# A two-layer kernel with routed experts: a later place for the third sequence's shared experts, and a group-wise scatter of layer 1's rows

## The chip, the core and the metric

The kernel runs on one core of one Trainium2 chip. The metric is the device time of one execution in microseconds (us). The engines that matter here are the TensorE (PE in the profile; PEld is its loading of weights), the VectorE (DVE), the ScalarE (ACT), the GpSimd (POOL) and the SyncE (SP), which only starts transfers. Each engine executes its own instructions in order, and waits for others by semaphores. [...]

## The reference

Four sequences of 1024 tokens of 256 numbers pass through two layers. In each, a mixer gives s and a feed-forward part gives g, both from the same normalized input, and x becomes x + s * silu(g):

```python
x = L0_attn_x
xn = _layernorm(x)
s = _L0_attn_ref(xn, ...)          # minGRU, a scan over the tokens
g = _silu(_L0_ffn_ref(xn, ...))    # 16 experts of 128 hidden, 4 of them per token
x = x + s * g
xn = _layernorm(x)
s = _L1_attn_ref(xn, ...)          # attention on cos(theta) * cos(xn)
g = _silu(_L1_ffn_ref(xn, ...))    # shared experts + 16 experts of 64 hidden, 4 per token
x = x + s * g
```

The two parts of layer 1 that the change touches are, with x standing for the normalized input:

```python
# attention of one sequence
proj = cos(theta) * cos(x)
out  = softmax(proj @ proj.T / sqrt(16)) @ proj @ W_c.T + b_c
# feed-forward of one sequence
shared = (silu(x @ shared_gate_w.T) * (x @ shared_up_w.T)) @ shared_down_w.T   # 512 hidden
routed = sum over the 4 chosen experts e of  w_e * (silu(x @ gate_e) * (x @ up_e)) @ down_e
g      = silu(shared + routed)
```

Attention and the shared experts of a sequence need nothing of the routed experts; the three meet in the last line of the layer only.

## The kernel before

**Tiles.** Rows are taken 128 at a time, one token to a partition. A sequence has 8 such tiles and is worked on in two halves of four tiles. All matrix products are in float32.

**Routed experts of layer 1.** The sequences form two groups, (0, 1) and (2, 3). For a group, `route1` (L895) normalizes the rows, writes them to `normed` in DRAM, computes the router's products and picks the four experts of each token. `places1` (L920) then gives each of its (token, expert) pairs a slot, so that the slots of one expert lie together. `dispatch1` (L923 to L945) reads the normalized rows back, half a sequence at a time (`t_half`, L938), adds the pairs' numbers (L939, L940), and scatters the rows into the slots in DRAM with `scattered` (L569 to L579): 16 indirect DMAs for each half sequence, all started by POOL (L574), 64 for a group. Loads run two halves ahead of the scatters (AHEAD = 2), and `t_half` takes one of the 8 buffers of a pool (tag "x", XB = 8) that serve the rows gathered in layer 0, the values of the attention and the results of the experts as well. `weights1` (L947) turns the weights of a group's pairs into weights by slot on DVE (L447, L454, L455).

`experts1` (L1166) goes through the slots of both groups, 20 quads of four tiles for each. `experts` (L588) loads a quad with ACT's queue (L613), transposes it (`turn`, L622, L626), multiplies with an expert's weights (`hidden`, L634), transposes (`turn_hidden`, L651) and multiplies again (`down`, L659). `store` scatters the results with indirect DMAs of POOL (L1192).

**Attention, shared experts, gating.** `prep1` (L954 to L1003) computes the cosines and the products of the values (L993, copied to `val` by ACT at L1000). `attend` (L1005 to L1108) is the attention of one sequence: scores (L1046), exponentials (L1058, L1062), products with the values (L1078); the last blocks are copied by DVE and ACT (L1103, L1105). `share` (L1114 to L1164) does the shared experts of one sequence: the two products with the 512 hidden (L1125), the sigmoid part on ACT (L460), two products on DVE (L461, L1135), the product back (L1141), then ACT's copy (L1161) and write to `shared` in DRAM (L1162). `gated1` (L1208 to L1261) waits for a group's results, loads `shared`, `attended` and the four results of each token, adds them up (L1231) and finishes the layer (L1246 to L1249).

**Order.** The order is written out at build time. `run(steps, us, beside)` emits one main stage step by step and moves a modelled clock on by `us` for each step; after each step it lets the side stages in `beside` emit those steps that are due by that clock. A side stage (`Beside`) is a generator that yields how long it wants to pause. So the modelled clock decides where side work stands among the main work on each engine; at run time the engines follow their orders and semaphores alone. `pool_free` is the modelled time at which POOL will have started all its indirect DMAs, at 1.27 us each (INDIRECT). `together` and `until` move the clock on without main work; `behind` puts what is emitted inside it behind all that has been emitted so far on each engine.

Layer 0's experts are the first main stage that matters here, with four side stages: `clearing` (zeros into the slots), `combined` (the last scan, and layer 0's gathers and gating, `combine0`, with the gathers at L716 and the gating at L782, L789 and L791), `routing` and `preparing`. `routing` holds, one after the other, the routes and places of group 0, those of group 1, and both dispatches. Then follow attention and shared experts of the sequences 0, 1 and 2, then all routed experts of layer 1, then the shared experts and the attention of sequence 3:

```python
others = [clearing, combined, routing, weighing]
for b in range(3):
    preparing = Beside(prep1(b + 1, "gu")) if b < 2 else Beside(())
    run(attend(b), ATTEND, [*others, preparing])
    run(share(b), SHARE, [*others, preparing])
    together(preparing)
```

Of the kernel before, what the change touches and what calls it, by code (L numbers as in the profile page):

```python
# [26 lines left out]
GROUPS = ((0, 1), (2, 3))  # L27
# [26 lines left out]
PAIR, ATTEND, SHARE, ROUTED = 0.81, 1.4, 2.6, 0.64  # L54
# [8 lines left out]
def two_layer_kernel(  # L63
# [33 lines left out]
    def halves(dram, b):  # L97
        return dram[b].rearrange("(c p) d -> p c d", p=P)
# [380 lines left out]
    G1 = len(GROUPS)  # L479
# [80 lines left out]
    def spent(us):  # L560

        clock[0] += us
# [282 lines left out]
    @contextmanager  # L845
    def behind():

        with ExitStack() as stack:
            engines = mybir.EngineType
            for engine in (engines.PE, engines.DVE, engines.Activation, engines.SP, engines.Pool):  # L850
                stack.enter_context(tc.issue_after(latest(engine)))
            yield
# [21 lines left out]
    def run(steps, us, beside=(), until=None):  # L874


        for i, _ in enumerate(steps, 1):
            clock[0] += us
            for other in beside:
                with behind():  # L880
                    other.advance(clock[0])
            if i == until:
                break
# [37 lines left out]
        placed1.append((yield from places(em1[:, tiles_of(h), :], G1 + h, WE1, "tp")))  # L921

    def dispatch1(h):  # L923
        while not clearing.done:
            yield PIECE
        row, top, _ = placed1[h]
        pieces = [(b, q) for b in GROUPS[h] for q in range(NQ)]
        n = NS * TOPK
        views = dram_disjoint_views(rows_in[G1 + h], len(pieces) * n)

        tokens = {}
        for i in range(-AHEAD, len(pieces)):
            if i + AHEAD < len(pieces):
                j = i + AHEAD
                tokens[j] = t = xpool.tile([P, NS, D + INFO], F32, tag="x", name="t_half", bufs=XB)
                ts = slice(j * NS, (j + 1) * NS)
                b, q = pieces[j]
                nc.gpsimd.dma_start(out=t[:, :, 0:D], in_=halves(normed, b)[:, q * NS : (q + 1) * NS, :])  # L938
                nc.gpsimd.tensor_copy(t[:, :, D : D + TOPK], top[:, ts, 0:TOPK])  # L939
                nc.gpsimd.tensor_copy(t[:, :, D + TOPK], result0[:, ts])  # L940
            if i >= 0:
                scattered(views[i * n : (i + 1) * n], tokens.pop(i), row, i * NS)
                while clock[0] < pool_free[0] - n * INDIRECT:
                    yield PIECE
        dispatched.add(h)  # L945
# [8 lines left out]
    def prep1(b, tag):  # L954

        if b < 2:
            while b not in turned:
                yield PIECE
            xnT = turned[b]
        else:  # L960
            while b not in routed_done:
                yield PIECE
            xnT = transposed_tile()
            nc.sync.dma_start(out=xnT.rearrange("p k s -> p (k s)"), in_=normedT[b])
            there = clock[0] + LANDING
            while clock[0] < there:
                yield PIECE
        if b == 1:

            projT = [work.tile([P, QUAD, D + INFO], F32, tag="q", name="projT", bufs=QB) for _ in range(KC)]  # L970
            projT = [t.rearrange("p i d -> p (i d)")[:, 0:S] for t in projT]
        else:
            projT = work.tile([P, KC, S], F32, tag="big_a", name="projT", bufs=1)
            projT = [projT[:, kc, :] for kc in range(KC)]
        for kc in range(KC):
            for cols in (slice(0, TB), slice(TB, S)):
                k = work.tile([P, TB], F32, tag="t", name="k", bufs=1)
                for _ in cos_reduced(projT[kc][:, cols], xnT[:, kc, cols], k, TWO_PI_NORMED):
                    pass
                yield 2 * PIECE  # L980
        for kc in range(KC):
            nc.scalar.activation(projT[kc], projT[kc], AF.Sin, bias=half_pi, scale=-1.0)
        yield PIECE
        for kc in range(KC):
            nc.vector.tensor_scalar(projT[kc], projT[kc], cth[:, kc : kc + 1], None, ALU.mult)
        yield 3 * SETTLED

        val = [xpool.tile([P, NS, D + INFO], F32, tag="x", name="val", bufs=XB)[:, :, 0:D] for _ in range(NQ)]
        for c in range(0, NT, 2):
            ps = bank(tag, 2)  # L990
            for i in range(2):
                for kc in range(KC):
                    nc.tensor.matmul(  # L993
                        ps[:, i * D : (i + 1) * D],
                        lhsT=projT[kc][:, (c + i) * P : (c + i + 1) * P],
                        rhs=wc_sb[:, kc, :],
                        start=(kc == 0),
                        stop=(kc == KC - 1),
                    )
            nc.scalar.copy(val[c // NS][:, c % NS : c % NS + 2, :], ps.rearrange("p (c d) -> p c d", d=D))  # L1000
            spent(1.7)
            yield PIECE
        ready[b] = xnT, projT, val  # L1003
# [162 lines left out]
    def experts1():  # L1166

        views = [dram_disjoint_views(r, n) for r, n in zip(results, NSLOT[G1:])]

        def target(q, xs):  # L1170

            info = xs[:, :, D:]
            own = slot_no[:, q * QUAD : (q + 1) * QUAD]
            nc.vector.scalar_tensor_tensor(
                info[:, :, 0:TOPK],
                info[:, :, 0:TOPK],
                -MARK,
                own.unsqueeze(2).to_broadcast([P, QUAD, TOPK]),
                ALU.add,
                ALU.is_gt,  # L1180
            )
            to_row = small.tile([P, QUAD, 1], F32, tag="to_row", name="to_row", bufs=1)
            nc.vector.tensor_reduce(to_row, info, AX.X, ALU.add)

            dest = small.tile([P, QUAD], I32, tag="dest", name="dest", bufs=6)
            nc.vector.scalar_tensor_tensor(dest, own, float(B * S * TOPK), to_row[:, :, 0], ALU.add, ALU.min)  # L1186
            return dest

        def store(g, q, o, dest):
            indirect(QUAD)  # L1190
            for i in range(QUAD):
                nc.gpsimd.indirect_dma_start(  # L1192
                    out=views[g - G1][QUAD * q + i],
                    out_offset=bass.IndirectOffsetOnAxis(ap=dest[:, i : i + 1], axis=0),
                    in_=o[:, i, :],
                    in_offset=None,
                )

        def begin(g):
            until(lambda: g - G1 in dispatched, routing, weighing)  # L1200

        def end(g):
            stored1[g - G1] = max(clock[0], pool_free[0]) + LANDING

        of_tiles = [of_tile for _, _, of_tile in placed1]
        return experts(range(G1, 2 * G1), of_tiles, we1_sb, WE1, P // 2, store, target, begin, end)

    def gated1(b):  # L1208
# [104 lines left out]
    def then(*steps):  # L1313
        for g in steps:
            yield from g

    def until(ready, *beside):

        while not ready():
            clock[0] += PIECE  # L1320
            for other in beside:
                with behind():
                    other.advance(clock[0])

    ready, turned, placed1, weights, dispatched, stored1 = {}, {}, [], [], set(), {}
    clearing = Beside(clears(10))
    combined = Beside(then(gru(xnTs[3], 3, ("side", "side"), True), *(combine0(g) for g in range(len(HALVES)))))
    routing = Beside(
        then(
            *(step for h, bs in enumerate(GROUPS) for step in (routes1(bs, "side"), places1(h))),  # L1330
            *(dispatch1(h) for h in range(len(GROUPS))),
        )
    )
    preparing = Beside(prep1(0, "side"))
    with behind():
        run(experts0(), PAIR, [clearing, combined, routing, preparing])
# [9 lines left out]
    nc.sync.dma_start(out=we1_sb, in_=w1)  # L1346
    combined.pace = routing.pace = 0.7
    weighing = Beside(weights1())
    others = [clearing, combined, routing, weighing]
    for b in range(3):  # L1350
        preparing = Beside(prep1(b + 1, "gu")) if b < 2 else Beside(())
        run(attend(b), ATTEND, [*others, preparing])
        run(share(b), SHARE, [*others, preparing])
        together(preparing)
    until(lambda: len(placed1) == len(GROUPS), *others)
    preparing = Beside(prep1(3, "gu"))

    gating = Beside(then(*(gated1(b) for b in range(B))), 1.7)
    with behind():
        run(experts1(), ROUTED, [routing, weighing, preparing, gating])  # L1360
    together(preparing, weighing)
    gating.pace = 1.0
    run(share(3), SHARE, [gating])
    run(attend(3), ATTEND, [gating])
    together(gating)

# [64 lines left out]
```

## Time and profile before

| what | time |
| --- | --- |
| median of five runs | 1479.96 us |
| lowest and highest of the five | 1464.4 and 1483.38 us |
| the profiled execution | 1485.71 us |
| its span on the core | 1483.7 us |

| engine | busy us | share of the span | instructions |
| --- | --- | --- | --- |
| PE | 1095.3 | 74% | 4928 |
| DVE | 648.9 | 44% | 1963 |
| POOL | 552.5 | 37% | 588 |
| ACT | 464.0 | 31% | 1030 |

In the profiled execution layer 0's gathers end at 776 us. Group 0 of layer 1 is scattered from 803 to 888 us, group 1 from 909 to 991 us. attend(2) starts at 1003 us and share(2) at 1051 us; the routed experts of layer 1 start at 1098 us. share(3) follows them from 1384 us on and attend(3) from 1427.5 us on. The last matmul ends at 1475.3 us.

The profile comes from one execution. It gives, for each engine, busy time and the groups of instructions that make it up; for each stretch of time, busy time, granted clock and DMA traffic; and, for every instruction, when it ran, how long its engine was idle before it, and what ended that idle time. The chain of waits follows the work that ended last back from the last instruction, at each step to what released it. "remote", in the chain "another core or an unknown queue", stands for an idle time whose end the profile can't put down to an instruction.

### The profile page before, as it was taken

How to read it: one execution, taken by the hardware profiler on the slowest of the kernel's cores; microseconds unless marked ns; L12 is line 12 of the kernel's file. 1: busy time of each engine (PE TensorE's matmuls, PEld its weight loads, DVE VectorE, ACT ScalarE, POOL GpSimd, SP SyncE). 2: the span in 40 equal slices, each digit the busy share in tenths (PEclk: the TensorE clock that was granted, in tenths of full speed). 3: DMA queues.
4: the chain of work that ended last, by engine and by line, in shares of the span. 5: the costliest groups of instructions: out<-in, count | busy, mean ns of one | idle time of the engine just before them, and what ended most of it. 6: DMA issues, size and time to landing. Idle time of an engine off the chain costs nothing.

```text
span 1483.7 us, 16138 instructions
## 1 busy us (share of the span) xinstructions
PE 1095.3 (74%) x4928; PEld 809.5 (55%) x4928; DVE 648.9 (44%) x1963; ACT 464.0 (31%) x1030; POOL 552.5 (37%) x588
## 2 busy tenths in 40 slices
PE   6537751399928999939688718319989898879997
PEld 4215321288827878626366504207667676667566
DVE  5813910233317853137958314111244333546585
ACT  3404420244414554302333301002225444434222
POOL 0570277300264000266243774750005555546300
PEclk9756775599959999968799759759999989879999
DMA  9982334288948959838254433320224456887681
GB/s 337 401 328 91 102 116 146 93 219 226 268 136 243 282 165 242 281 104 198 73 199 157 158 106 116 117 79 15 85 78 147 158 163 195 274 274 235 211 269 54
DMA packets 154290, 264.81 MB, mean 178 GB/s; under 512 B 14176, under 2 KB 118752, under 8 KB 152928
## 3 DMA queue, kind: packets, MB, share of 16 engines
q1 hardware_dynamic: 106976, 137.18, 30.8%
q0 software_dynamic: 27264, 75.86, 15.0%
q10 hardware_dynamic: 19968, 50.75, 10.2%
q8 instruction: 43, 0.70, 0.2%
q14 instruction: 39, 0.32, 0.1%
HBM read 119.34 MB, written 144.39 MB: 178 GB/s over the span
## 4 chain that ended last, share of the span: by engine, by line
PE 39%; another core or an unknown queue 18%; DVE 15%; issue 11%; POOL 9%; DMA 4%; ACT 2%; ACTq 0%; POOLq 0%; DVEq 0%; SPq 0%
PE gu L634 9%; POOL results L1192 6%; PE acc L659 5%; PE acc L1078 4%; PE tp L622 3%; POOL r L716 3%; PE gu L1125 2%; PE acc L1141 2%; PE mm L1046 2%; PE mm L1125 2%; DMA xs<-rows_in 2%; PE tp L651 1%; PE acc L288 1%; DVE stats L191 1%
## 5 line engine op out<-in xcount | busy, mean ns | idle before, releaser
L716 POOL DMA_INDIRECT r<-rows_out,row x128 | 127.6, 997 | 371.8 <-DMA g_half<-in_x_dram 146.9
L634 PE MATMUL gu<-w_sb,xT 128*128 x1280 | 255.7, 346 | 3.2 <-issue 3.1
L1192 POOL DMA_INDIRECT results<-o,dest x160 | 159.0, 994 | 243.2 <-DVE dest L1186 171.3
L634 PEld LDWEIGHTS gu<-w_sb,xT 128*128 128x128 f32 x1280 | 208.9, 206 | 19.8 <-issue 4.4
L461 DVE SCALAR_TENSOR_TENSOR h<-sg,gu 128x256 f32<-128x256 f32 (+1 forms) x160 | 56.3, 352 | 359.8 <-ACT sg L460 311.9
L659 PE MATMUL acc<-w_sb,hT 128*128 (+1 forms) x640 | 182.4, 408 | 2.2 <-ACT hT L653 1.3
L574 POOL DMA_INDIRECT rows_in<-x_half,row x128 | 128.3, 1002 | 144.9 <-issue 95.2
L622 PE MATMUL tp<-ident,xs 128*128 128x128 f32 x640 | 108.8, 296 | 75.2 <-ACT xT L626 41.0
L1078 PE MATMUL acc<-val,es 128*128 128x256 f32 x512 | 132.9, 406 | 33.0 <-ACT es L1058 22.2
L626 ACT COPY xT<-tp 128x512 f32<-128x512 f32 x160 | 94.0, 587 | 166.6 <-PE tp L622 60.1
L622 PEld LDWEIGHTS tp<-ident,xs 128*128 128x128 f32 x640 | 79.1, 150 | 114.8 <-issue 51.6
L574 POOL DMA_INDIRECT rows_in<-t_half,row x128 | 125.8, 983 | 39.3 <-issue 36.7
L1078 PEld LDWEIGHTS acc<-val,es 128*128 128x128 f32 x512 | 100.8, 204 | 59.9 <-ACT es L1058 24.4
L659 PEld LDWEIGHTS acc<-w_sb,hT 128*128 128x128 f32 (+1 forms) x640 | 114.1, 198 | 31.6 <-issue 19.8
L1141 PE MATMUL acc<-w_sb,act 128*128 128x256 f32 x256 | 64.9, 403 | 57.0 <-DVE act L1135 37.8
L651 PE MATMUL tp<-ident,h 128*128 128x128 f32 (+1 forms) x320 | 65.9, 290 | 52.7 <-issue 40.0
L460 ACT ACTIVATE sg<-gu 128x256 f32<-128x256 f32 (+1 forms) x160 | 53.1, 332 | 161.0 <-PE gu L634 95.7
L1141 PEld LDWEIGHTS acc<-w_sb,act 128*128 128x128 f32 x256 | 51.0, 202 | 77.2 <-DVE act L1135 36.5
L651 PEld LDWEIGHTS tp<-ident,h 128*128 128x128 f32 (+1 forms) x320 | 40.2, 133 | 68.2 <-issue 48.6
L1046 PE MATMUL mm<-projT 128*128 128x512 f32 (+3 forms) x192 | 72.9, 504 | 0.0
L1125 PE MATMUL mm<-xnT,w_sb 128*128 128x512 f32 x128 | 63.0, 616 | 9.3 <-DVE act L461 9.3
L653 ACT COPY hT<-tp 128x256 f32<-128x256 f32 (+1 forms) x160 | 58.4, 365 | 27.2 <-remote 8.4
(224 smaller groups left out, 1503.0 us busy)
## 6 DMA issues: line engine op xcount, KB each, us to landing
rows_in<-zeros SPq DMA_DIRECT2D x20, 1044.0 KB
xs<-rows_in ACTq DMA_DIRECT2D x40, 522.0 KB
xs<-rows_in SPq DMA_DIRECT2D x40, 512.0 KB
rows_out<-o ACTq DMA_DIRECT2D x40, 512.0 KB
r<-results SPq DMA_DIRECT2D x32, 512.0 KB
rows_in<-zeros SPq DMA_DIRECT2D x1, 12288.0 KB
rows_in<-zeros SPq DMA_DIRECT2D x1, 8192.0 KB
w_sb<-in_w_dram SPq DMA_DIRECT2D x4, 1536.0 KB
```

What stands on the lines that cost most here:

```text
L574: nc.gpsimd.indirect_dma_start(out=view, out_offset=bass.IndirectOffsetOnAxis(ap=row[:, c0 + s, k : k + 1], axis=0), in_=tokens[:, s, :], ...
L622: nc.tensor.transpose(tp[:, at : at + P], xs[:, j % per * 2 + i, kc * P : (kc + 1) * P], ident)
L626: nc.scalar.copy(xT.rearrange("p i k t -> p (i k t)"), tp)
L634: nc.tensor.matmul(ps[:, i * 2 * hid : (i + 1) * 2 * hid], lhsT=xT[:, i, kc, :], rhs=w_sb[:, bass.ds(off + kc * 2 * hid, 2 * hid)], start= ...
L651: nc.tensor.transpose(tp[0:hid, i * P : (i + 1) * P], h[:, i, :], ident)
L659: nc.tensor.matmul(ps[:, i * D : (i + 1) * D], lhsT=hT[0:hid, i * P : (i + 1) * P], rhs=w_sb[0:hid, bass.ds(expert(2 * j + i) + 4 * hid, D ...
L716: nc.gpsimd.indirect_dma_start(out=r[:, k, :], out_offset=None, in_=rows_out[g], in_offset=bass.IndirectOffsetOnAxis(ap=row[:, c, k : k + ...
L1046: nc.tensor.matmul(ps[:, at:TB], lhsT=projT[kc][:, t * P : (t + 1) * P], rhs=projT[kc][:, q * TB + at : (q + 1) * TB], start=(kc == 0), st ...
L1078: nc.tensor.matmul(av[s // 2][:, (s % 2) * D : (s % 2 + 1) * D], lhsT=es[:, s * P : (s + 1) * P], rhs=val[t // NS][:, t % NS, :], start=(t ...
L1125: nc.tensor.matmul(ps, lhsT=w[:, kc, j * P : (j + 1) * P], rhs=xr[:, kc, :], start=(kc == 0), stop=(kc == KC - 1),)
L1141: nc.tensor.matmul(ys[s // 2][:, (s % 2) * D : (s % 2 + 1) * D], lhsT=h[:, s * P : (s + 1) * P], rhs=ds1_sb[:, j, :], start=(j == 0 and s ...
L1192: nc.gpsimd.indirect_dma_start(out=views[g - G1][QUAD * q + i], out_offset=bass.IndirectOffsetOnAxis(ap=dest[:, i : i + 1], axis=0), in_=o ...
```

## The change

Three things are changed. First, `dispatch1` is taken out of `routing` and becomes a side stage of its own, `dispatching`. Group h is dispatched as soon as the slots are cleared, layer 0's side work (`combined`, the last gathers in it) has been emitted and the places of group h have been emitted; before, both dispatches came behind the routes and places of both groups. Second, share(2) is left out of the loop over the first three sequences. Third, it is emitted behind the routed experts of layer 1, ahead of share(3). The number of instructions stays the same.

```diff
     def dispatch1(h):
-        while not clearing.done:
+
+        while not (clearing.done and combined.done and len(placed1) > h):
             yield PIECE
...
         def begin(g):
-            until(lambda: g - G1 in dispatched, routing, weighing)
+            until(lambda: g - G1 in dispatched, dispatching, weighing)
...
             *(step for h, bs in enumerate(GROUPS) for step in (routes1(bs, "side"), places1(h))),
-            *(dispatch1(h) for h in range(len(GROUPS))),
         )
     )
+    dispatching = Beside(then(*(dispatch1(h) for h in range(len(GROUPS)))))
...
-    others = [clearing, combined, routing, weighing]
+    others = [clearing, combined, routing, dispatching, weighing]
     for b in range(3):
         preparing = Beside(prep1(b + 1, "gu")) if b < 2 else Beside(())
         run(attend(b), ATTEND, [*others, preparing])
-        run(share(b), SHARE, [*others, preparing])
+        if b < 2:
+            run(share(b), SHARE, [*others, preparing])
         together(preparing)
...
     with behind():
-        run(experts1(), ROUTED, [routing, weighing, preparing, gating])
+        run(experts1(), ROUTED, [dispatching, weighing, preparing, gating])
     together(preparing, weighing)
     gating.pace = 1.0
-    run(share(3), SHARE, [gating])
+    for b in (2, 3):
+        run(share(b), SHARE, [gating])
     run(attend(3), ATTEND, [gating])
     together(gating)
```

## The prediction

> **What bounds the kernel now.** I read the busy table of the page, then the busy time by stretches of time, then the chain of waits and the timelines of ACT, PE and POOL between 735 and 1110 us, where the moved work lies. Two stages matter: POOL's issue of layer 1's row scatters, and what follows the routed experts.
>
> Busy time by stretches (columns: stretch, its length, busy us and instruction count of PE, PEld, DVE, ACT, POOL, then granted clock, DMA share, GB/s):
>
> ```profile
> 803.00:888.00 85.00, 41.01 (x166) 31.44 (x163) 32.32 (x108) 17.93 (x37) 65.78 (x70) 0.70 0.41 143
> 909.00:991.00 82.00, 35.24 (x102) 20.95 (x100) 10.96 (x22) 2.99 (x5) 62.81 (x67) 0.75 0.35 124
> 1050.00:1092.00 42.00, 41.44 (x131) 24.50 (x129) 17.93 (x33) 7.68 (x13) 0.00 (x0) 1.00 0.19 63
> 1387.00:1422.00 35.00, 35.00 (x108) 20.22 (x108) 19.18 (x34) 6.73 (x12) 4.81 (x5) 1.00 0.81 262
> 1422.00:1475.00 53.00, 52.31 (x226) 39.04 (x224) 34.21 (x70) 17.43 (x54) 0.00 (x0) 1.00 0.46 151
> ```
>
> In the first two, group 0 and group 1 are scattered, and PE works less than half the time though it has share(1), the projection of values and the end of attend(1) to do. In the third, share(2) now runs, and PE is full. In the last two, share(3) and attend(3) run after the experts, and PE is full too.
>
> The chain of waits (start, us, what) says what holds PE in the first two:
>
> ```profile
> 844.36 4.99 PE gu L993 x16
> 849.64 34.04 another core or an unknown queue
> 884.29 9.91 another core or an unknown queue
> ...
> 926.00 7.67 another core or an unknown queue
> 933.72 18.89 another core or an unknown queue
> 952.66 43.35 another core or an unknown queue
> ...
> 999.60 3.78 PE acc L1141 x8
> 1003.38 3.58 PE mm L1046 x8
> ```
>
> The ACT timeline names the waiting instructions (start, duration, last bracket: idle time before, releaser):
>
> ```profile
> 883.70 0.59 ACT L1000 COPY val<-gu 128x512 f32<-128x512 f32 x1 [33.74 <-remote]
> ...
> 933.69 0.60 ACT L460 ACTIVATE sg<-mm 128x512 f32<-128x512 f32 x1 [7.12 <-remote]
> 952.63 0.60 ACT L460 ACTIVATE sg<-mm 128x512 f32<-128x512 f32 x1 [18.34 <-remote]
> 996.03 0.60 ACT L460 ACTIVATE sg<-mm 128x512 f32<-128x512 f32 x1 [42.80 <-remote]
> ```
>
> Each of these reads a PSUM tile that PE had filled long before; with one core there is no other core to wait for. What arrives late is PE's completion signal, and it does so while POOL issues indirect DMAs without a pause: group 0's 64 at one per 1.27 us from 803.29 to 887.6, group 1's 64 from 909.0 to 990.9. The wait grows with the time since the run of scatters began: 7 us at 25 us into it, 18 at 44, 43 at 87. In group 0's run the last handoff that passes is at about 40 us, and the next release comes at 883.70, 80 us in. When POOL stops, PE is full again (47.00 of 47 us from 1003).
>
> **Moving share(2).** Before it stands between attend(2), whose last matmul ends at 1050.85, and the first transpose of the experts at 1097.61: 46.76 us. The PE timeline shows the end of it:
>
> ```profile
> 1087.82 3.62 PE L1141 MATMUL acc<-w_sb,act 128*128 128x256 f32 x16
> 1097.61 1.97 PE L622 MATMUL tp<-ident,xs 128*128 128x128 f32 x8 [6.17 <-DMA xs<-rows_in]
> ```
>
> So PE works on share(2) for 40.6 us (1050.85 to 1091.44), then waits 6.17 us for the experts' first rows. That wait does not go with share(2): the experts' rows are loaded from ACT's queue (L613), behind ACT's last copy. After the change that is attend(2)'s L1105 (0.59 us), and the load takes the 4.77 us that the chain shows: a new gap of 5.7 us, between 0 (the load gets ahead of the copy) and 6.2. Gain: 46.76 - 5.7 = 41.0 us. The experts cannot be held by their data when they start 41 us sooner: the scatter of group 1 ends at 990.9, 60 us before 1050.85, and POOL does nothing from then to 1111.35. The weights of group 1 (DVE, 12 instructions of 0.42 us, 5.0 us) then lie beside attend(2), where DVE is busy 3.14 of 47 us.
>
> Afterwards the same 64 products of L1125 and 64 of L1141 run behind the experts. The price is that of share(3): its second half runs from 1406.86 to 1427.50, 20.64 us with no idle time, so 41.3 us for two halves. Nothing covers it: PE is busy 35.00 of 35 us there, and attend(3) follows at full PE. The 41.3 us are paid in full; the lower bound is share(2)'s present 40.6, the upper some 3 us more if its DVE work (16 instructions of 0.69 us, 11 us) lies badly with gated1's (in that stretch DVE is busy 19.18 of 35). Its 8 + 4 ACT instructions (0.60 us each, 7 us) have room. gated1(2) must now wait until share(2)'s two writes have landed (SP's loads of shared for it, and gated1(3)'s loads queued behind them, wait too); but DVE has 125 us of PE time in the tail for work that now fits in 84, so the end stays attend(3)'s last matmul plus the 8.4 us of finishing (1475.3 to 1483.7). Sum of this part: -41.0 + 41.3 = +0.3, between -6 and +4.
>
> **Group 0's scatter.** Before, group 0 is dispatched after both groups' routing, and three loads of rows (L938) stand on POOL ahead of the first scatter. POOL's timeline:
>
> ```profile
> 786.56 0.81 POOL L938 DMA_DIRECT2D t_half<-normed  x1 [10.54 <-DVE pen L327]
> ...
> 792.45 0.80 POOL L938 DMA_DIRECT2D t_half<-normed  x1 [4.74 <-DVE cden L347]
> ...
> 801.80 0.75 POOL L938 DMA_DIRECT2D t_half<-normed  x1 [8.23 <-DVE y L782]
> ...
> 803.29 1.05 POOL L574 DMA_INDIRECT rows_in<-t_half,row  x1 [0.16 <-POOL t_half L940]
> ```
>
> The three loads take buffers that the last three pieces gathered in layer 0 give back (L782, ends near 786.3, 792.2 and 801.5). In the new order one load takes an earlier piece's buffer, the second the one free at 786.3, and scatters stand between the second and the third. So the first scatter comes at about 788.5, 13 to 15 us sooner, and the last near 874 instead of 887.6. The instructions on POOL are the same in number. places1(1) (first matmul L362 at 896.73) stands on PE behind the value projection, so what counts is when L362 runs; group 1's scatter follows it by 12 us (909.0), and share(1)'s remainder and attend(2) follow that.
>
> How much of the 13 us comes through? The releases should keep their distance from the start of the run of scatters. The last handoff passes at 40 to 44 us, now about 831, and the next at 80 us, now about 869. At 831 PE stands 18 us of work before the 849.6 where it stopped in the profile (attend(1) ended at 844.15 and L993 at 849.4). It does that after 869, to 887, then the remaining value products (3.78 and 2.08 us): L362 near 893, 4 us earlier. If instead nothing more is caught than before, it is 13 us earlier; if attend(1) is caught 30 us in (where the second run already shows waits of 7 to 18 us), 27 us and more of work is left at 874 and L362 comes at up to 910, 13 us late. I take -4, with both ends for the range. The 12 weight instructions of group 0 (5.0 us), now ahead of share(1)'s second half on DVE, fall into waits of 18 to 43 us and cost 0; without that cover 5.
>
> One rule speaks against any effect here. The Trainium skill, "SBUF — State Buffer", section "Who interferes with whom", says that PE and ACT never wait on anyone for SBUF, only GpSimd and DVE share a port pair. If that were all, POOL's scatters would not hold PE's handoffs, their shift would be worth 0, and the whole would be +0.3. The 42.80 us row above does not look like that; no other row here separates a memory port from a late signal.
>
> **Sum.** +0.3 - 4 = -3.7 us on the profiled execution of 1485.71 us (span 1483.7), 1482.0. That execution is 5.75 us above the median of 1479.96, so the median becomes 1476. The five times before lie between 1464.4 and 1483.38, so 1% (15 us) is about what can be told from no change.
>
> **Rivals.** A, faster: the end of the scatter alone sets L362, so the whole 13 us come through, and the experts' first load is hidden too: -13 to -18, 1462 to 1467. For it: 883.70 and 996.03 both lie at the end of a run. Against it: attend(1) is not done when the signals begin to stay out. B, slower: the last 25 us of attend(1) and the route of sequence 3, many short PE-ACT-DVE handoffs, fall 15 us deeper into the run. It decides if attend(1) has not ended by 880 us; L362 then comes 13 us late or more, group 1's run and its 80 us with it, and with share(1)'s first half (918 before) caught as well up to 25 us: 1493 to 1505. For it: waits of 7 us appear 25 us into a run. Against: attend(1) ran 817 to 842, 14 to 39 us into its run, with one stall of 4.46 us. C, the new conditions do not act: the gathers and L782 set the first scatter as before (three loads waited for them), leaving only +0.3: 1480.
>
> **Chances.** Forecast 0.46 (own range 1466 to 1489), A 0.22, B 0.24, C 0.08. Faster by over 1% (under 1465): most of A and an edge of the forecast, 0.23; slower (over 1495): most of B and an edge, 0.25; else 0.52. For 8 in 10 the range takes A to 1455 (A's end less half of the spread of the times) and B to 1503.
>
> **What would show it.** Right: experts' first transpose 5 to 7 us after attend(2)'s last matmul; share(2) and share(3) as some 81 us of full PE after the experts; first scatter near 788; L362 near 893; attend(2) starting near 999. A would show L362 near 884, B one after 905 and attend(1) ending after 870. The forecast is wrong if the scatter costs PE nothing once it is moved, or if PE idles in the tail because gated1 holds buffers that share(2) needs.

## The result and the profile after

| | before | after |
| --- | --- | --- |
| median of all executions | 1483.6 us (79 runs) | 1478.24 us (42 runs) |
| lowest and highest | 1460.22 and 1504.78 | 1463.77 and 1493.83 |
| profiled execution | 1485.71 us, span 1483.7 | 1473.43 us, span 1471.7 |

The ratio of after to before is 1.0003, with a 95% interval of 0.9981 to 1.0025: no change that can be told. This ratio leaves out executions more than 1.5% above the fastest of their kernel (48 of 79 before, 9 of 42 after), which here cuts into an ordinary spread with a standard deviation of some 9 us; the medians of all executions stand at 0.9964. The forecast of -3.7 us (0.9975) lies between the two and just outside the interval. Its two terms were both wrong in size, in opposite directions, as the profile after shows.

Busy time by stretches, after (columns as before: stretch, length, busy us and count of PE, PEld, DVE, ACT, POOL, granted clock, DMA share, GB/s): the scatter of group 0, that of group 1, then share(2) and share(3) behind the experts.

```profile
785.00:873.00 88.00, 52.14 (x220) 39.31 (x218) 42.84 (x151) 23.26 (x50) 68.92 (x74) 0.81 0.47 163
895.00:978.00 83.00, 37.38 (x110) 21.91 (x108) 16.21 (x33) 5.38 (x9) 63.15 (x67) 0.74 0.33 114
1328.00:1372.00 44.00, 41.86 (x131) 24.46 (x130) 21.24 (x36) 8.72 (x15) 5.17 (x6) 1.00 0.36 118
1372.00:1416.00 44.00, 41.84 (x123) 23.74 (x123) 28.71 (x54) 8.46 (x15) 0.00 (x0) 0.96 0.64 203
```

PE still works only half of the time beside the scatters. The tail is not quite full: PE misses 2 us in each of the last two stretches, where before it was busy 35.00 of 35.

The chain of waits, after (start, us, what):

```profile
852.61 25.68 another core or an unknown queue
878.31 0.60 ACT val L1001
...
878.96 5.40 PE gu L994 x12
884.35 0.43 PE tp L362 x2
...
911.08 8.66 another core or an unknown queue
919.79 14.06 another core or an unknown queue
933.89 42.66 another core or an unknown queue
976.57 0.60 ACT ysh L1162
```

The same unexplained waits stand at the same kind of place as before, the two ahead of L362 having become one of 25.68 us instead of 34.04 and 9.91. ACT's timeline names them:

```profile
878.31 1.07 ACT L1001 COPY val<-gu 128x512 f32<-128x512 f32 x2 [25.39 <-remote]
...
933.87 0.60 ACT L460 ACTIVATE sg<-mm 128x512 f32<-128x512 f32 x1 [13.51 <-remote]
976.57 0.60 ACT L1162 ACTIVATE ysh<-acc 128x512 f32<-128x512 f32 x1 [42.10 <-remote]
```

POOL's last scatter of group 0 ends at 872.8, that of group 1 at 977.8; both long waits end near the end of a run of scatters, not at a fixed time from its start (878.31 is 92.8 us behind the first scatter of its group, 976.57 is 81.0).

Marks of the two timelines, in us (the first column is the end of layer 0's gathers on POOL):

| | gathers end | first scatter | L362 | attend(2) ends | experts start | last L659 ends | last matmul ends |
| --- | --- | --- | --- | --- | --- | --- | --- |
| before | 776.0 | 803.3 | 896.7 | 1051.0 | 1097.6 | 1387.9 | 1475.3 |
| after | 773.7 | 785.5 | 884.2 | 1032.2 | 1036.0 | 1328.5 | 1463.2 |

From these differences: -2.3 us up to the gathers, which the change doesn't touch; -10.2 from the gathers to L362 and -6.3 from there to the end of attend(2), together -16.5 for the dispatch; -42.8 from attend(2) to the experts, +2.2 in the experts and +47.3 behind them, together +6.7 for the move of share(2). The sum is -12.1, in two single executions of kernels that scatter by some 9 us each: the one of before took 2.1 us more than the median of its kernel, the one of after 4.8 us less.

### The profile page after: what moved, and what is told of

It is laid out like the page before. It is cut to its first block, busy times and chain, and to the rows that moved or that the text cites. A ratio compares the mean times of both kernels' runs of the same rounds, so it can differ in the third digit from the quotient of the medians.

```text
span 1471.7 us, 16132 instructions
## 1 busy us (share of the span) xinstructions
PE 1084.6 (74%) x4928; PEld 804.9 (55%) x4928; DVE 649.3 (44%) x1963; ACT 463.2 (31%) x1030; POOL 558.8 (38%) x588
## 3 DMA queue, kind: packets, MB, share of 16 engines
q10 hardware_dynamic: 19968, 50.75, 10.2%
## 5 line engine op out<-in xcount | busy, mean ns | idle before, releaser
L634 PE MATMUL gu<-w_sb,xT 128*128 x1280 | 252.7, 343 | 0.8 <-issue 0.8
L659 PE MATMUL acc<-w_sb,hT 128*128 (+1 forms) x640 | 183.6, 410 | 0.7 <-ACT hT L653 0.7
L659 PEld LDWEIGHTS acc<-w_sb,hT 128*128 128x128 f32 (+1 forms) x640 | 114.9, 200 | 30.2 <-issue 17.7
```

What stands on the lines that cost most here:

```text
L634: nc.tensor.matmul(ps[:, i * 2 * hid : (i + 1) * 2 * hid], lhsT=xT[:, i, kc, :], rhs=w_sb[:, bass.ds(off + kc * 2 * hid, 2 * hid)], start= ...
L659: nc.tensor.matmul(ps[:, i * D : (i + 1) * D], lhsT=hT[0:hid, i * P : (i + 1) * P], rhs=w_sb[0:hid, bass.ds(expert(2 * j + i) + 4 * hid, D ...
```

## Experiments

Times on different chips were of two kinds: the kernel before took some 1170 us on four chips and 1480 to 1500 us on three, the latter like the recorded comparison. So each comparison below is with runs of before on the same chip, and each says which kind of chip it was: with PE's signals late (as in the profiles shown so far), or not. A signal is the semaphore update by which an engine tells a waiting one that its work is done.

**The two halves of the change alone.** Only share(2) moved (shown against the changed kernel; the lists of side stages have `routing` again in place of `dispatching`):

```diff
 def dispatch1(h):
-    while not (clearing.done and combined.done and len(placed1) > h):
+    while not clearing.done:
...
+            *(dispatch1(h) for h in range(len(GROUPS))),
-    dispatching = Beside(then(*(dispatch1(h) for h in range(len(GROUPS)))))
```

> Only share(2) is moved; the dispatch stays as before. Theory (the move is a wash: some 41 us less ahead of the experts, 41 us plus a loss to gated1's DVE work more behind them): the median stays within 5 us of the kernel before; the experts' first transpose comes 41 to 47 us sooner than before; share(2) and share(3) take 82 us if nothing is in their way, 87 us if gated1's DVE bursts cost what they cost in the changed kernel (87.7 us there, against two times 20.64 x 2 = 82.6). Rival (the move itself gains, the dispatch nothing): 8 to 12 us under before, as in the changed kernel's profile.

Only the dispatch changed (against the changed kernel):

```diff
-        if b < 2:
-            run(share(b), SHARE, [*others, preparing])
+        run(share(b), SHARE, [*others, preparing])
...
-    for b in (2, 3):
-        run(share(b), SHARE, [gating])
+    run(share(3), SHARE, [gating])
```

> Only the dispatch is changed; share(2) stays in the loop. Theory (what moves the time is the earlier scatter): L362 comes near 884 us instead of 897, attend(2) starts 10 to 20 us sooner, and the median is 5 to 12 us under before. Rival (the starved stretch takes it back, the shift is run-to-run scatter): within 4 us of before, with attend(2) ending at its old place.

Both fell on a chip without late signals: before 1171.21 us, the move alone 1188.04 us (ratio 1.014, interval 1.0103 to 1.0178), the dispatch alone 1167.63 us (0.9969, 0.9943 to 0.9995). The move was expected to be a wash and lost 17 us; the dispatch gained 3.6 us, less than its theory and within what its rival allowed. L362 stood at 669.4 and 667.8 there; the numbers expected for it belonged to the other kind of chip.

**The kernel before and the changed kernel on such chips.**

> The kernel before, unchanged, for its profile on the chip of the first experiments. The executions there were 300 us shorter than those of the first profile, with a granted clock of 0.94 instead of 0.85. Theory: PE's completion signals are not late on this chip; the scatters of group 0 and group 1 then end near 800 us with PE busy over 80% beside them, and no wait of ACT for a remote releaser over 5 us. Rival: another part of the kernel is faster there, and the waits of 18 to 43 us under the scatters are still in it.

> The changed kernel, unchanged. Theory (share(2) in the loop hid the end of group 1's scatter, which holds the results' scatters on POOL when the experts start 40 us sooner): on the chip of the first experiments 0.5 to 1.2% over before, with the experts stopped for 15 to 30 us some 36 us after their start, and share(2) + share(3) taking 84 to 88 us. On a chip with late signals: within 1% of before. Rival (only gated1's DVE bursts cost): 0.3 to 0.5% over before, no stop in the experts.

The kernel before took 1172.34 us in its profiled execution, and the changed kernel 1180.78 us against 1169.95 us (ratio 1.0084, 1.0051 to 1.0117). Busy time beside the whole run of scatters (632.9 to 806.8 us), kernel before on a chip without late signals:

```profile
632.90:806.80 173.90, 164.38 (x644) 112.66 (x642) 78.55 (x228) 46.73 (x111) 133.44 (x143) 0.99 0.49 166
```

POOL issues the same 128 scatters at the same 1.27 us each, and PE is busy 95% of the time instead of some 45%; no wait in this profile is put down to a remote releaser. So the scatters as such, with their bytes and their place, do not hold PE.

With late signals, the waits are not the dispatch's alone. In the trace of before 25 waits of 3 us or more are put down to a remote releaser, 349 us in all (some beside each other), and each begins in a run of at least 12 of POOL's indirect DMAs with less than 1 us between one and the next. Layer 0's scatters and gathers are among these runs; ACT's timeline:

```profile
286.20 0.59 ACT L626 COPY xT<-tp 128x512 f32<-128x512 f32 x1 [26.93 <-remote]
...
664.90 0.60 ACT L1058 ACTIVATE es<-mm 128x512 f32<-128x512 f32 x1 [21.37 <-remote]
```

The first wait began in a run of 80 scatters (172.0 to 276.6 us), the second in one of 32 gathers (620.7 to 661.4). The results' scatters, in runs of at most 12, go with no such wait. The two profiles of before differ by 313 us: 164 up to the end of layer 0's gathers (776.0 against 611.6), 128 from there to the experts, 21 in the experts.

Because PE is not held, attend(2) ends 40 us before the scatter of group 1, and the experts then run into it. POOL's and DVE's timelines of the changed kernel on such a chip (start, duration, then idle time before and releaser):

```profile
795.35 0.96 POOL L574 DMA_INDIRECT rows_in<-t_half,row  x1 [0.30 <-issue]
796.62 0.96 POOL L1193 DMA_INDIRECT results<-o,dest  x1 [0.30 <-issue]
```

```profile
802.94 0.69 DVE L677 COPY o<-acc 128x512 f32<-128x512 f32 x1 [6.27 <-DMA results<-o,dest]
```

The experts start at 760.8, but their first results are scattered at 796.62, directly behind the last row of group 1. With all buffers of o full, DVE waits, and the experts stand still from 799.5 to 816.9. PE is idle for 4.1 us of that and does the value projection of sequence 3 (L994) in the rest. In the run of the move alone, where group 1's scatter ended 16 us later, the stop is idle time, as DVE's and PE's timelines there show:

```profile
819.21 0.69 DVE L677 COPY o<-acc 128x512 f32<-128x512 f32 x1 [20.19 <-DMA results<-o,dest]
```

```profile
820.24 3.75 PE L994 MATMUL gu<-wc_sb,projT 128*128 128x256 f32 x8 [18.02 <-DVE xs L1175]
```

From the first transpose to the last L659 the changed kernel takes 287.8 us instead of 269.5; with -44.2 us ahead of the experts and +45.4 behind them, this makes the loss in the profiles. (They differ by 19.3 us, the profiled execution being the slowest of the changed kernel's eight; the medians differ by 10.8.) Of the 18.3 us in the experts PE's idle time makes 8; its busy time makes the other 10 (255.43 us instead of 245.02, at a granted clock of 0.90 instead of 0.94), and why that is so was not tried.

**Holding back the end of group 1's scatter.** The last 16 of its 64 scatters are issued one behind each quad of results (`HELD` is 3, `stores` lists the quads whose results have been emitted, `one_scattered` starts a single scatter):

```diff
             if i >= 0:
-                scattered(views[i * n : (i + 1) * n], tokens.pop(i), row, i * NS)
-                while clock[0] < pool_free[0] - n * INDIRECT:
+                t = tokens.pop(i)
+                for m in range(n):
+                    while h and i >= HELD and len(stores) <= (i - HELD) * n + m:
+                        yield PIECE
+                    one_scattered(views[i * n + m], t, row, i * NS, m)
+                while clock[0] < pool_free[0] - n * INDIRECT and not (h and i >= HELD):
                     yield PIECE
```

> The changed kernel, with the last 16 of group 1's 64 scatters held back and issued by POOL one behind each of the experts' first 16 quads of results; the same scatters and rows. Theory (on the chips of the experiments the experts' stop near 800 us is the results' scatters standing behind group 1's on POOL, which makes DVE wait 6.3 us for a buffer of o): the stop goes or shrinks to under 6 us, first transpose to last L659 takes 270 to 278 us instead of 287.8, median 8 to 14 us under the changed kernel, 0.0 to 0.3% over before. Rival (the stop is the value projection of sequence 3, or the late rows of the experts themselves): a stop of 15 us stays and the median with it.

Without late signals: 1171.05 us against 1172.19 (0.9984, 0.9953 to 1.0014). The stop is gone (first transpose to last L659: 275.9 us, with PE idle for 21.3 us of it instead of 32.4), and with it the loss: 1.0% under the changed kernel's ratio. The value projection, the rival, stands in the same place and takes 8.6 us instead of 13.0. The theory held: on these chips the stop is POOL's order.

**Spreading the gating.** `gating.pace = 2.0` instead of 1.0 beside share(2) and share(3), first on the changed kernel, then on the one with held scatters:

> The changed kernel, with gated1's steps spread twice as thin beside share(2) and share(3) (pace 2.0 instead of 1.0), and at 1.0 again beside attend(3). Theory (the 5 us by which share(2) and share(3) are longer than twice 41.3 come from DVE working off a burst of gated1 ahead of L1136): the two take 82 to 84 us instead of 87.7 and the median is 3 to 6 us lower, if the gating left over fits beside attend(3). Rival (it fits not, or the loss is the lower clock): no change, or 3 to 10 us more after the last matmul.

> As the kernel with interleaved scatters, and with gated1 at pace 2.0 beside share(2) and share(3) as in the experiment on gating. Theory (both losses are separate and add up): tail from the last L659 to the last matmul 129 us, experts 270 to 278 us, median 0 to 0.5% under before. Rival (one loss covers the other, or moving share(2) costs something else): still 0.3% or more over before.

Without late signals: 1178.77 us (1.0059, 1.0035 to 1.0084), and 1168.21 us (0.9990, 0.9964 to 1.0017). The tail, from the last L659 to the last matmul, fell to 129.1 us from 132.8, and to 130.1 from 131.6 (87.4 before the change), but the times can't be told from those of the kernels with pace 1.0. The tail's loss has this cause, by the lengths in the profile; as a gain in time it was not shown.

**Pauses of POOL.** Twelve small memsets behind every four scatters of the dispatch:

```diff
-                scattered(views[i * n : (i + 1) * n], tokens.pop(i), row, i * NS)
+                t = tokens.pop(i)
+                for s in range(0, n, TOPK):
+                    scattered(views[i * n + s : i * n + s + TOPK], t[:, s // TOPK :, :], row, i * NS + s // TOPK)
+                    for _ in range(12):
+                        nc.gpsimd.memset(rest, 0.0)
```

> The changed kernel, with 12 small memsets of POOL (about 2 us) behind every four scatters of the dispatch; the same scatters, rows and bytes. Theory (PE's completion signals come late only while POOL issues indirect DMAs back to back; a pause lets them through): no wait of ACT for PE over 10 us between 785 and 1000 us, PE over 70% busy there, experts start 40 us or more sooner, median 30 to 80 us lower. Rival (it is the scattered bytes, or the DMA queue, that hold PE): the scatter only gets longer, waits of 20 to 40 us stay, median equal or up to 30 us higher.

This fell on a chip without late signals, where there is nothing to cure: 1291.64 us (1.1031, 1.099 to 1.1072). The run of scatters then ends at 889.6 us and the experts, which had started at 763.2, stand still until 919.7. The memsets also did not stay where they were written but were issued one by one and in blocks of 12 us. In the next form each is put behind the instruction before it on POOL, and for group 0 alone:

```diff
+                    with tc.issue_after(latest(mybir.EngineType.Pool)):
+                        scattered(views[i * n + s : i * n + s + TOPK], t[:, s // TOPK :, :], row, i * NS + s // TOPK)
+                    for _ in range(12 if h == 0 else 0):
+                        with tc.issue_after(latest(mybir.EngineType.Pool)):
+                            nc.gpsimd.memset(rest, 0.0)
```

> The changed kernel with 12 small memsets (some 3 us) behind every four scatters of group 0, kept in place; group 1 as before. On a chip where PE's signals come late. Theory (the signals pile up while POOL issues indirect DMAs and drain in a pause): the longest wait for a remote releaser between the first scatter and the last of group 0 is under 8 us instead of 25.4, and L362 comes before the last scatter of group 0, at 850 to 870 us instead of 884, though POOL's run is 48 us longer. Rival (a count of scatters or bytes makes them late, pauses do not help): waits of 20 us or more stay and L362 comes after the longer run, at 920 us or later. On a chip without late signals both give no wait.

Again a chip without late signals: 1242.12 us against 1170.08 (1.0602, 1.0551 to 1.0653), and no such wait. The same kernel once more:

> As the earlier run of this kernel, which fell on a chip without late signals. With late signals, theory: longest wait for a remote releaser during group 0's scatters under 8 us instead of 25.4, L362 at 850 to 870 us. Rival: waits of 20 us or more stay, L362 at 920 us or later. Without late signals: 6% over before, no such wait.

This time the signals were late: 1463.06 us against 1497.55 (0.9799, 0.9728 to 0.9869, two executions). Busy time, first beside the paused scatter of group 0, then beside the unpaused one of group 1:

```profile
785.00:930.00 145.00, 139.76 (x582) 100.47 (x581) 80.02 (x267) 46.98 (x117) 112.89 (x252) 0.99 0.34 118
930.00:1015.00 85.00, 21.30 (x92) 16.64 (x92) 8.62 (x25) 6.30 (x14) 64.68 (x83) 0.54 0.49 165
```

With pauses PE is busy 96% of the time, with the rest of attend(1), share(1) and attend(2) in this stretch; L362 stands at 837.2 (earlier than the theory had it), attend(2) ends at 926.4 instead of 1032.2. No wait there comes from a remote releaser, and ACT waits at most 4.6 us for PE. Without pauses, 10 us later in the same execution, PE is busy 25%, its granted clock falls to 0.54, and ACT waits up to 22.51 us for a remote releaser. Not all of this is late signals: the results stand behind group 1's scatter here too, and without late signals the same kernel has PE busy 36% in this place:

```profile
758.00:843.00 85.00, 30.59 (x168) 24.50 (x168) 21.95 (x59) 19.89 (x37) 64.87 (x82) 0.67 0.55 184
```

What carries the reading is group 0: the same scatters without pauses left PE busy 52.14 of 88 us in the changed kernel, with a wait of 25.39 us. The theory holds: the same scatters and bytes, broken up, do not make the signals late. Pauses also make the scatters rarer on average; a steady, slower issue was not tried, so that it is the break and not the rate is not shown.

**The halves once more, beside the whole.**

> Only share(2) moved, on a chip with late signals. Theory (the gain of the changed kernel there is the earlier scatter alone, the move loses some 6 us in gated1's DVE bursts): 3 to 10 us over before, tail from the last L659 to the last matmul 132 to 136 us, no stop in the experts. Rival (the move gains, the dispatch nothing): 4 to 12 us under before. On a chip without late signals: 1.4% over before, as measured.

> Only the dispatch changed, on a chip with late signals. Theory: L362 near 884, attend(2) going on near 987, share(2) ending near 1074 instead of 1091, median 8 to 16 us under before. Rival: within 4 us of before. On a chip without late signals: 0.3% under before, as measured.

> The changed kernel beside the two halves of the change on the same chip. Theory: its difference to before is the sum of theirs within 4 us; with late signals 3 to 8 us under before, without them 10 us over. Rival (the parts do not add up): more than 6 us from the sum.

A chip without late signals again. Before 1170.08 us; the move 1.0118 (1.0074 to 1.0163), the dispatch 0.9970 (0.9944 to 0.9997), the whole 1.0087 (1.005 to 1.0123). The parts add up to 0.9% there. The dispatch alone once more, this time with late signals:

> Only the dispatch changed. With late signals, theory: from the end of layer 0's gathers to the end of attend(2) 259 to 262 us instead of 275, from there to the last matmul 424 us as before (431 in the changed kernel), median 10 to 16 us under before. Rival: within 4 us of before. Without late signals: 0.3% under before, as measured.

1487.79 us against 1497.55: 9.8 us less by the medians, 0.9971 (0.9932 to 1.0011) by the ratio, so not told from none by the latter. In the profile, gathers' end to the end of attend(2) took 261.7 us (275.0 before), as expected. From there to the last matmul it took 433.3 us where 424 was expected: the experts took 297.3 us, against 290.3 in the profile before. So the experts' length scatters by 7 us between executions with late signals, and of the move's +6.7 only the part in the tail is safe (1.6 to 6.0 us over 41.3 in seven profiles with pace 1.0 and no pauses, on both kinds of chip).

**Earlier loads for the experts.** Their first three loads are started from ACT's queue in the middle of attend(2), here on the kernel with held scatters, and in the middle of share(2) on the dispatch change alone:

```diff
...
+        if b == 2:
+            run(scores, ATTEND, others, until=20)
+            until(lambda: 0 in dispatched, *others)
+            routed1 = experts1()
+            with behind():
+                next(routed1)
...
```

> As the kernel with interleaved scatters, with the experts' first three loads of rows started from ACT's queue in the middle of attend(2) instead of behind its last copy. Theory (the 4 to 6 us between the last matmul ahead of the experts and their first transpose are that load alone): this gap falls under 1 us, median 3 to 6 us under the kernel with interleaved scatters, that is 0.4 to 0.7% under before. Rival (the next loads, or POOL, then set the pace): gap closed, median unchanged.

> As the kernel with the dispatch change alone (share(2) stays in the loop), with the experts' first three loads started in the middle of share(2). Theory: the gap of 6 us ahead of the first transpose closes, and with the 0.3% of the dispatch change the median is 0.6 to 0.9% under before. Rival: the gap closes and the experts wait for their next rows instead, 0.2 to 0.4% under before.

Both ran with late signals: 1456.61 and 1462.0 us against 1483.85 (0.9819, 0.9773 to 0.9864; 0.9838, 0.9784 to 0.9891). In both the first transpose follows the last matmul with no gap (1013.2 behind 1013.4, 1088.5 behind 1088.7, the ends being modelled). In the first, group 1's unbroken run is 16 scatters shorter, ends at 959.2, and attend(2) goes on at 967.5: again some 8 us behind POOL's last scatter, as in the changed kernel (977.8 and 986.7). That brings the end of attend(2) to 1013.2 from 1032.2. The gains are larger than expected for chips without late signals, which these runs don't show.

**Short pauses.** Three memsets (about 1 us) behind every four scatters of both groups, on the kernel with the dispatch change and the early loads:

> The kernel with the dispatch change and the early loads (share(2) in the loop), with three small memsets (about 1 us) behind every four scatters of both groups. Theory (a pause of POOL lets PE's signals through, and share(2) in front of the experts hides the longer run): with late signals no wait for a remote releaser over 10 us between the first scatter and attend(2), experts start 60 us or more sooner than before, median 30 to 80 us under before; without late signals the run of scatters ends near 820 us, the experts stop for under 15 us, median between 0.6% under and 0.6% over before. Rival (a pause of 1 us is too short to drain, only one of 3 us is long enough): with late signals waits of 15 us or more, within 20 us of the kernel without pauses.

Without late signals: 1161.62 us against 1169.73 (0.9945, 0.9919 to 0.9972). The run of scatters ends at 822.1, and the experts stop for 15.4 us (824.0 to 839.4), just over what was expected; PE is busy for 11.1 us of that, mostly with the value projection.

> As the earlier run of this kernel, which fell on a chip without late signals (0.5% under before there). With late signals, theory: no wait for a remote releaser over 10 us between the first scatter and attend(2), experts start 60 us or more sooner than before, median 30 to 80 us under before. Rival (1 us is too short to drain): waits of 15 us or more, within 20 us of the kernel without pauses. Without late signals: 0.3 to 0.8% under before, as measured.

With late signals: 1359.72 us against 1481.39 (0.9201, 0.9148 to 0.9254), more than expected. Without the pauses this kernel stood at 0.9838, on another chip. Busy time beside the scatters (788.3 to 987.5):

```profile
785.00:895.00 110.00, 109.10 (x443) 76.35 (x442) 66.36 (x220) 37.29 (x84) 86.44 (x129) 1.00 0.44 152
895.00:1000.00 105.00, 97.88 (x430) 69.23 (x429) 42.31 (x100) 35.64 (x78) 83.75 (x122) 0.97 0.51 171
```

and the only remote releaser that the list of waits names between 785 and 1010 us (engine, line, us in total, times, longest):

```profile
ACT val L1009 <- remote: 9.7, 2, 5.1
```

Both of these waits begin at 998 us or later, in an unbroken run of 14 of the results' scatters. A pause of 1 us in 6 is enough here. The experts start at 960.8 instead of 1097.6. From the end of layer 0's gathers to the experts it takes 190.3 us with late signals and 184.2 without, where the kernel before took 321.6 and 193.4: in this stage 6 us are left of the 128 that the late signals cost. The 204 us that are left between the two profiles of this kernel lie in layer 0, whose indirect DMAs have no pauses (160 us), and in the experts (38 us). This version is faster than the kernel before on both kinds of chip, and its ratios are below those of the changed kernel (1.0003 and 1.0084).

## Why the prediction went as it did

**Ahead of the experts: right.** The gain of 41.0 us came as 42.8. The gap to the first transpose was 3.7 us, not 5.7; the PE timeline after:

```profile
1028.62 3.62 PE L1079 MATMUL acc<-val,es 128*128 128x256 f32 x16
1035.95 1.97 PE L622 MATMUL tp<-ident,xs 128*128 128x128 f32 x8 [3.71 <-DMA xs<-rows_in]
```

It was also right that the experts could not be held by group 1's scatter, but only because the signals were late: 977.8 lies 58 us before 1036.0. The step looked at the row as fixed. Where PE is not starved, attend(2) ends first, and the move costs 15 to 17 us.

**Behind the experts: the size was off.** 41.3 us were predicted, with 3 more as the upper end; it was 47.3. The step that failed set DVE's work for the whole tail against the whole tail's length. DVE executes in order, and gated1's L1232 come in bursts of up to nine ahead of a product that PE waits for. PE's timeline after:

```profile
1369.55 1.99 PE L1142 MATMUL acc<-w_sb,act 128*128 128x256 f32 x8 [2.14 <-DVE act L1136]
...
1391.64 2.76 PE L1142 MATMUL acc<-w_sb,act 128*128 128x256 f32 x8 [2.04 <-DVE act L1136]
1394.18 2.85 PE L1126 MATMUL mm<-xnT,w_sb 128*128 128x512 f32 x4
```

The two waits make 4.2 of the 6 us; behind the second, four products take 2.85 us instead of 1.88, and the granted clock of the stretch is 0.96. In six more profiles of kernels with the move (pace 1.0, no pauses) the tail grew by 42.9 to 45.4 us, so the loss is not chance, but the 6 us are its upper end.

**The dispatch: the mechanism was right, its share was off.** The first scatter came at 785.5 (788.5 predicted) and the last of group 0 at 872.8 (874). But L362 came at 884.2 and not near 893: rival A's mark. The step that failed is that the releases keep their distance from the start of the run, so that 18 us of attend(1) would be left behind at 831. In fact attend(1) ended at 843.1 and the first values at 848.3, 58 and 63 us into the run, because a handoff to ACT still passed at 840 (others at 852 and, to DVE, at 861). The profile before already held such a one, in DVE's timeline, which the prediction did not read:

```profile
857.11 0.69 DVE L1103 COPY sv<-acc 128x512 f32<-128x512 f32 x1 [18.81 <-remote]
...
872.50 0.17 DVE L346 TENSOR_SCALAR cden<-cden 128x8 f32<-128x8 f32 x1 [2.52 <-remote]
```

The first line is a release by PE 54 us into the run, where the prediction had none between 40 and 80. In the second DVE waits for a result of its own, 2.52 us where the same handoff takes 0.04 on a chip without late signals; so it is not PE's signals alone that come late. What sets the last release is the end of the unbroken issue: where a wait of 3 us or more outlasted it, in before, after and three other profiles with late signals, it ended 4.4 to 8.3 us behind it. Single releases came before it (883.70 in before, 976.57 in after). Thus most of the shift came through: counted from the end of the gathers, the last scatter of group 0 came 12.5 us sooner and L362 10.2 (10.3 and 10.0 in the two other profiles with this dispatch, share(2) in the loop and late signals). Up to the end of attend(2) it was 6.3 us more, with share(1) further ahead of group 1's run (3.0 and 3.6 in the two others). The dispatch term measured -16.5 in the profile after, -13.3 to the same mark in the run of the dispatch alone, and -9.8 by that run's medians (whose ratio tells it neither from -4 nor from none), against -4.

**The sum.** -4 + 0.3 predicted; -16.5 + 6.7 in the profiles (and -2.3 ahead of both), and -5.4 by the medians of all executions. That the total came near is two errors that met. Rival A was right about L362 but not about the total, since the move took part of it back; B did not occur (attend(1) ended long before 880); C did not (the first scatter moved by 18 us).

**The rule.** The Trainium skill's "SBUF — State Buffer", section "Who interferes with whom", says that PE and ACT never wait on anyone for SBUF. The runs neither contradict nor test that: PE waited for ACT's copies (30.63 us ahead of L994 at 878.96), and these waited for a signal (25.39 us, 42.10 us). Where the signals were not late, PE was busy 164.38 of 173.90 us beside the same scatters, as the rule would have it.

## What to carry to other kernels

A wait whose releaser the profile can't name, and that ends when another engine stops issuing, may come from that engine's issue: break the issue up as a test before moving work around it. Before taking a resource as free because its last use ended long ago, ask whether that use still ends first when the stage ahead of it gets faster. In a tail where one engine is full, compare bursts with the slack of one handoff, not sums with sums.

## What the runs showed of the hardware

The same program took some 1170 us on four chips and 1480 to 1500 us on three. On the latter, ACT waited up to 43 us for PE's completion signals while POOL issued indirect DMAs, scatters or gathers, at one per 1.27 us without a break (25 waits of 3 us or more in the trace of before), and no wait of 3 us or more was seen while it issued the same scatters with a break of about 1 us after every four. DVE's handoffs to itself took 1.0 to 2.5 us there (862 to 875 us in the profile before) instead of 0.04 or less. The scatters' own completions were not seen to be late: the landing recorded for the last row of group 1 stands at 979.1 us in the profile after, 1.3 us behind the end of its issue, while PE's signals still came 4.5 and 6.6 us after that (983.57, 985.70). The trace of before holds 9,623 records of semaphore updates from the chip with late signals and 17,353 from one without; whether the recording has a part in the delay, and why the chips differ, was not tried and stays open.
